# Routed expert tiles in half-tile slots (34 tiles instead of 36), and a new order in the end stage

## The chip, the core and the metric

The kernel runs on one core of one Trainium2 chip. The metric is the device time of one execution in microseconds; a run's time is the median of its executions. TensorE (PE) multiplies, and loads its stationary operand through a port of its own (PEld). VectorE (DVE), ScalarE (ACT) and GpSimd (POOL) work elementwise. SyncE (SP) issues most of the DMA transfers.

## What is computed

One transformer block on x of 2048 tokens by 512 features, all in float32. xn = layernorm(x). The output is x + attention(xn) + ffn(xn).

The attention is differential: 16 heads, two causal softmax maps for each head, a filter along the tokens by a real Fourier transform, a root-mean-square norm over each head, and a projection. The feed-forward part is a mixture of eight experts with two chosen for each token, and a shared expert of twice an expert's width:

```python
topk_w, topk_idx = jax.lax.top_k(scores, K)            # K = 2
topk_w = topk_w / jnp.sum(topk_w, axis=-1, keepdims=True)
h = jnp.einsum('th,ehi->eti', x, w1)                   # i = 352
g = jnp.einsum('th,ehi->eti', x, w3)
y_all = jnp.einsum('eti,eih->eth', jax.nn.silu(h) * g, w2)
...
shared = jax.nn.silu(x @ sw1) * (x @ sw3) @ sw2        # width 704
return y + shared
```

## The kernel before, in words

There are four stages. The first normalises the tokens, forms the values, and routes. Each token gets two slots, one for each of its experts. The slots of one expert stand together, in tiles of 128 (P); an expert's last tile may be partly empty. So 4096 slots and 8 experts need at most NS = 32 + 7 = 39 tiles. NR = 36 of them are always computed, and three more only under a condition (the branch on `more`). Which expert owns tile j is read at run time from `owner` (L452 to L458).

The second stage makes queries and keys and computes the shared expert for the first four token tiles.

The third, `middle`, is the long one. It interleaves two streams of work on PE by hand. One is attention: for each of eight head groups and four query chunks it does the scores (ps_s, L772), the exponentials on ACT (L785), the mask on POOL (L790), the products with the values (ps_o, L812), the sums of the probabilities on DVE (L829), and the closing steps (ps_sum, ps_ot, ps_st). The other is the generator `experts`, which first finishes the shared expert, then goes over the 36 routed tiles. A planner calls `work()` so often that the units of work done keep pace with the attention stream: it compares worked / (work_all - left) with the share of the stream, with left = 11.0.

For tile j the generator does, on PE, the transposition of the 128 gathered token rows (ps_x, L160), the two up products (xh in `up_first`, xg in `up_third`, both L169), the transposition of the gated result (ps_u, L192) and the down product (xy, L202). The down product of tile j stands one step later, after the xg of tile j + 1. ACT scales the result into y_sb (L211), and SP stores it in ys (L214).

The weights of an expert are 1408 KB for the up products (wu) and 768 KB for the down product (wd). There are two places for each. After the xg of tile j, SP issues the load of wu for tile j + 2 into the place just freed (L142); after the down product of tile j - 1, it issues wd for tile j + 1 (L145). After the last routed tiles the same places take the shared expert's weights for the last stage.

The last stage, `ending`, computes the shared expert for the last token tile (wh, L232; tanh into ws on ACT, L242; wy, L270), the filter's products (ps_r and ps_z, L1091) with additions on DVE, and the norm and the projection of 16 token tiles in eight pairs (`Pair`, `prepared`, ps_tr L1211, po L1219). The products of the filter beyond the first few need DVE's L1136 and L1137, which stand in DVE's order after the first ws of this stage. The program's memory is reused between stages: the first ws lies where buffers of `middle` lay. Gathers on POOL (L1075) add the two rows of ys of each token to the result.

DVE, PE, ACT, POOL and SP all run in the order in which the instructions stand, in `middle` and (without SP) in `ending`. "Tile j" below is the j-th routed tile; tiles count from 0.

Of the kernel before, what the change touches and what calls it, by code (L numbers as in the profile page):

```python
# [19 lines left out]
P = 128  # L20
# [22 lines left out]
NS = T * TOP // P + NX - 1  # L43
NR = NS - 3
# [13 lines left out]
C_ID, C_RANK, C_ROW, C_TOK = 0, 128, 136, 176  # L58
# [5 lines left out]
def block_kernel(  # L64
# [33 lines left out]
    rows = cst[:, C_ROW : C_ROW + NS]  # L98
# [4 lines left out]
    owner = cpool.tile([P, NS], I32, name="owner")  # L103
# [43 lines left out]
    def routed(j):  # L147
        return wex[bass.ds(nc.values_load(owner[0:1, j : j + 1], engines=[SP], min_val=0, max_val=NX - 1), 1)]

    def expert(mp, fps, yp=None, stores=2, by_scalar=False):  # L150
# [14 lines left out]
        def up_half(w, xT, i, name):  # L165
            dst = bank([P, FI], name)
            for c in range(NE):
                o = (2 * c + i) * FI
                nc.tensor.matmul(dst, xT[:, c, :], w[:, o : o + FI], start=(c == 0), stop=(c == NE - 1))  # L169
            return dst  # L170
# [27 lines left out]
        def down_products(pairs):  # L198
            y = bank([P, E], "xy")
            for n, (w, uT) in enumerate(pairs):  # L200
                for ic, (_, m) in enumerate(FCH):
                    nc.tensor.matmul(  # L202
                        y, uT[:m, ic, :], w[:m, ic * E : (ic + 1) * E],
                        start=(n == 0 and ic == 0), stop=(n == len(pairs) - 1 and ic == NF - 1),
                    )
            return y
# [9 lines left out]
        def down(pairs, *to):  # L216
            stored(down_products(pairs), *to)
# [61 lines left out]
    with ExitStack() as pools:  # L279
# [152 lines left out]
        nc.vector.tensor_scalar(n_int, before[:, NT, :], float(P - 1), None, ALU.add)  # L432
        nc.vector.tensor_scalar(n_int, n_int, -P, None, ALU.bitwise_and)
        ends = [l1.tile([P, NX], F32, name=f"ends{i}") for i in range(2)]
        nc.vector.tensor_copy(ends[0], n_int)
        cur = 0
        for d in (1, 2, 4):
            nc.vector.tensor_copy(ends[1 - cur][:, :d], ends[cur][:, :d])
            nc.vector.tensor_add(ends[1 - cur][:, d:], ends[cur][:, d:], ends[cur][:, : NX - d])
            cur = 1 - cur  # L440
        first = l1.tile([P, NX], F32, name="first")
        nc.vector.memset(first[:, 0:1], 0.0)
        nc.vector.tensor_copy(first[:, 1:], ends[cur][:, : NX - 1])
        at = l1.tile([P, NT, NX], F32, name="at")
        nc.vector.tensor_add(at, before[:, :NT, :], first.unsqueeze(1).to_broadcast([P, NT, NX]))
        for k in range(TOP):
# [3 lines left out]

        past = l1.tile([P, NS, NX], F32, name="past")
        nc.vector.tensor_tensor(  # L452
            past, rows.unsqueeze(2).to_broadcast([P, NS, NX]),
            ends[cur].unsqueeze(1).to_broadcast([P, NS, NX]), ALU.is_ge,
        )
        own = l1.tile([P, NS], F32, name="own")
        nc.vector.tensor_reduce(own, past, AX.X, ALU.add)
        nc.vector.tensor_scalar(owner, own, float(NX - 1), None, ALU.min)  # L458
        nc.vector.tensor_scalar(more, ends[cur][0:1, NX - 1 : NX], NR * P + 0.5, None, ALU.is_gt)

# [86 lines left out]
        for n, us in enumerate(chunks(xnT[:, :, : EARLY * P], u_last)):  # L547
            if n == 0:
                pm = lps.tile([P, 2, P], F32, tag="x", name="ps_most")
                for i in range(2):  # L550
                    nc.tensor.transpose(pm[:1, i, :], most[:, i : i + 1], ident)
                line = l1.tile([1, 2], F32, name="line")
                nc.vector.tensor_reduce(line, pm[:1], AX.X, ALU.max)
                prod = l1.tile([1, 1], F32, name="prod")
                nc.vector.tensor_mul(prod, line[:, 0:1], line[:, 1:2])
                nc.vector.tensor_scalar(calm, prod, BOUND / (D * SCALE), None, ALU.is_le)
        for t in range(EARLY):
            stored(result(us, t), ysh[t], 0.5, nc.gpsimd)

    def middle(general):  # L560


        with ExitStack() as pools:
# [29 lines left out]
            def experts():  # L593
# [7 lines left out]
                for t0 in range(EARLY, NT - 1, TQ):  # L601
# [24 lines left out]
                    if last:  # L626
                        es.append(routed(1))
                        fetch_up(es[1], 1, nc.sync)
# [11 lines left out]
                yield 0.6  # L640
                for j in range(NR):
                    if j > 0:
                        late = [(w_sb[(j - 1) % 2][1], turned_back(u))], ys[(j - 1) * P : j * P, :], wcol[:, j - 1 : j]
                    half = up_first(w_sb[j % 2][0], xT)
                    yield 2.9 if late else 2.4
                    u = up_third(w_sb[j % 2][0], xT, half)
                    if j + 2 < NR:
                        xr.append(rows_of(j + 2))

                    es.append(routed(j + 2) if j + 2 < NR else wex[NX + j + 2 - NR : NX + j + 3 - NR])  # L650
                    fetch_up(es[j + 2], j % 2, nc.sync)
                    yield 2.4
                    if j + 1 < NR:
                        xT = transposed(xr.pop(0))
                    if late:
                        down(*late)
                        fetch_down(es[j + 1], (j + 1) % 2, nc.sync)
                    if j == 1:
                        shared.append(True)
                    if late:  # L660
                        yield 3.2
                late = [(w_sb[j % 2][1], turned_back(u))], ys[j * P :][:P], wcol[:, j : j + 1]
                yield 0.5
                down(*late)
                yield 2.8
# [265 lines left out]
            work_all = (NT - 1 - EARLY) * ((2 * SCH - 1) * 3.45 / TQ + 5.2) + NR * 8.5  # L931
            left = 11.0
# [108 lines left out]
    def ending():  # L1041
# [3 lines left out]
        with tc.tile_pool(name="tail1", bufs=1) as t1, tc.tile_pool(name="tail", bufs=2) as tp, tc.tile_pool(  # L1045
# [110 lines left out]
            z = at(5, vd, 14)  # L1156
# [32 lines left out]
            def prepared(n):  # L1189

                z, i, by = ((z0, 0, 1.0), (z1, 2, ROOT), (z0, 1, COS8), (z1, 3, COS8 * ROOT))[n // 2]
                if n == 2:
                    nc.vector.tensor_sub(u0, u0, v0)
                    turned(z1, u0)
                elif n == 4:
                    scaled(v1[:, 0], dv[:, 1], TAN8, dv[:, 0])
                    scaled(v1[:, 1], dv[:, 0], -TAN8, dv[:, 1])

                    nc.vector.tensor_add(z0[:, 0], u1[:, 0], v1[:, 1])
                    nc.vector.tensor_sub(z0[:, 1], u1[:, 1], v1[:, 0])  # L1200
                elif n == 6:
                    nc.vector.tensor_sub(u1[:, 0], u1[:, 0], v1[:, 1])
                    nc.vector.tensor_add(u1[:, 1], u1[:, 1], v1[:, 0])
                    turned(z1, u1)
# [53 lines left out]
            nc.vector.tensor_sub(dv, z, dv)  # L1258
# [3 lines left out]
            for n in range(NT // 2):  # L1262
# [4 lines left out]
                if n == 0:  # L1267
                    stored(y, ysh[NT - 1], 0.5)
# [16 lines left out]
    with tc.If(nc.values_load(more[0:1, 0:1], min_val=0, max_val=1) > 0):  # L1285

        with tc.tile_pool(name="before_more", bufs=1) as gap, tc.tile_pool(name="more", bufs=2) as mp, tc.tile_pool(
# [4 lines left out]
            for j in range(NR, NS):  # L1292
                w = mp.tile([P, WCOL], F32, tag="w", name="w")
                nc.sync.dma_start(w, routed(j).rearrange("o p w -> p (o w)"))
# [11 lines left out]
                u = up(w[:, :WUP], transposed(x))  # L1306
                down([(w[:, WUP:], turned_back(u))], ys[j * P : (j + 1) * P, :], pairs[:, 1:])
# [11 lines left out]
def _tables():  # L1319
# [7 lines left out]
    cst[:, C_ROW : C_ROW + NS] = P * np.arange(NS)  # L1327
# [91 lines left out]
```

## Time and profile before

| | |
|---|---|
| median of 3 runs | 1362.34 us (1362.26 to 1364.04) |
| the profiled execution, its own time | 1361.8 us |
| its span | 1360.1 us |
| PE busy | 1322.2 us, 97% of the span |
| DVE, ACT, POOL busy | 1002.6, 691.8, 615.9 us |
| TensorE clock granted, mean | 0.996 |
| DMA | 206.65 MB, 152 GB/s mean |
| xh and xg (L169), 288 instructions each | 91.8 and 94.1 us busy |
| xy (L202), 216 instructions | 100.9 us busy |
| routed tiles, first xh to last xg | 598.1 to 1232.4 us of the span |

How to read it: a span is the time from the first to the last instruction that the profiler recorded. The execution's own time is 1.7 us longer. A float32 matrix product appears as two instructions for one of the program, so four products of 128x352 stand as x8. Matrix products are pipelined and their ends are modelled, so the start of one to the start of the next tells more than the length of one.

### The profile page before, as it was taken

The numbers are of one execution on the slowest core, as the hardware profiler recorded it, in microseconds if no ns is written. First come the engines' busy times: TensorE is split into PE (matmuls) and PEld (weight loads), VectorE is DVE, ScalarE is ACT, GpSimd is POOL, SyncE is SP. The second block draws the span as 40 slices with busy tenths as digits, with TensorE's granted clock in tenths as the row PEclk, the third lists the DMA queues.
The fourth block names the chain that finished last, engine by engine and source line by source line (L and its number), as shares of the span: only waits on it lengthen the run. The fifth ranks groups of instructions, "written<-read, shape, count | busy, mean of one in ns | idle before, by whom it ended". The sixth has DMA issues, their size and how long they took to land.

```text
span 1360.1 us, 20623 instructions
## 1 busy us (share of the span) xinstructions
PE 1322.2 (97%) x7480; PEld 613.6 (45%) x7480; DVE 1002.6 (74%) x1339; ACT 691.8 (51%) x853; POOL 615.9 (45%) x673
## 2 busy tenths in 40 slices
PE   7999999999999999999999999999999999998998
PEld 3444444333443444444444444444444454445544
DVE  7048882287668778767886878997788779776785
ACT  2311110265656566565666666666666666661321
POOL 0003420012220323227884986795369529731764
PEclk9999999999999999999999999999999999999999
DMA  9406662200210122236565666466566555557997
GB/s 378 175 16 177 200 202 90 89 12 31 67 52 30 38 77 80 75 114 182 180 216 168 197 192 191 148 211 202 164 183 215 193 178 182 179 169 259 191 223 153
DMA packets 75024, 206.65 MB, mean 152 GB/s; under 512 B 12200, under 2 KB 12656, under 8 KB 69536
## 3 DMA queue, kind: packets, MB, share of 16 engines
q1 hardware_dynamic: 62032, 177.56, 40.2%
q0 software_dynamic: 11216, 23.31, 8.5%
q10 hardware_dynamic: 1664, 4.36, 0.9%
q8 instruction: 62, 1.02, 0.3%
q14 instruction: 50, 0.41, 0.1%
HBM read 161.29 MB, written 43.89 MB: 151 GB/s over the span
## 4 chain that ended last, share of the span: by engine, by line
PE 65%; DVE 7%; POOL 5%; DMA 2%; issue 1%; ACT 1%; DVEq 0%; ACTq 0%; POOLq 0%
PE ps_o L812 16%; PE ps_s L772 12%; PE wh L232 9%; PE xy L202 6%; PE xg L169 6%; PE xh L169 5%; PE wy L270 4%; DVE sum L829 2%; PE ps_sum L838 2%; POOL pt L790 2%; DMA wu<-in_wex_dram 1%; PE ps_ot L850 1%; PE ps_u L192 1%; PE po L1219 1%; PE ps_x L160 1%
## 5 line engine op out<-in xcount | busy, mean ns | idle before, releaser
L829 DVE TENSOR_TENSOR sum<-sum,pt 128x1024 f32<-128x1024 f32 (+3 forms) x576 | 621.8, 1128 | 35.2 <-ACT pt L785 23.3
L785 ACT ACTIVATE pt<-ps_s 128x1024 f32<-128x1024 f32 x544 | 527.1, 1022 | 182.1 <-PE ps_s L772 125.7
L790 POOL TENSOR_SCALAR_AFFINE_SELECT pt<-pt 128x256 f32<-128x256 f32 x256 | 168.7, 683 | 385.5 <-ACT pt L785 372.0
L812 PE MATMUL ps_o<-pt,vd 128*32 128x512 f32 (+3 forms) x2560 | 268.4, 534 | 2.9 <-POOL pt L790 2.9
L772 PE MATMUL ps_s<-qS,kS 64*128 64x512 f32 (+3 forms) x1280 | 204.0, 406 | 1.7 <-DVEq L1285 1.6
L772 PEld LDWEIGHTS ps_s<-qS,kS 64*128 64x128 f32 x1280 | 97.4, 185 | 176.6 <-issue 98.3
L232 PE MATMUL wh<-xnT,wu 128*128 128x512 f32 (+1 forms) x352 | 151.9, 579 | 0.0
L812 PEld LDWEIGHTS ps_o<-pt,vd 128*32 128x32 f32 x2560 | 66.9, 109 | 124.8 <-issue 107.8
L522 PE MATMUL ps_x<-xnT,wqk_sb 128*128 128x512 f32 x256 | 110.5, 593 | 0.0
L202 PE MATMUL xy<-wd,uT 128*128 128x512 f32 (+1 forms) x216 | 100.9, 603 | 7.1 <-DVE rcp L853 7.1
L475 POOL DMA_INDIRECT who<-pairs,slot x32 | 33.7, 1053 | 141.8 <-DVE pairs L472 100.6
L232 PEld LDWEIGHTS wh<-xnT,wu 128*128 128x128 f32 x352 | 64.8, 191 | 73.2 <-issue 57.9
L169 PE MATMUL xg<-wu,xT 128*128 128x352 f32 x288 | 94.1, 470 | 0.0
L169 PE MATMUL xh<-wu,xT 128*128 128x352 f32 x288 | 91.8, 462 | 0.3 <-DMA wu<-in_wex_dram 0.2
L867 POOL TENSOR_TENSOR vd<-o_n 128x128 f32<-128x128 f32 x60 | 63.0, 1069 | 63.8 <-DVE o_n L858 63.7
L522 PEld LDWEIGHTS ps_x<-xnT,wqk_sb 128*128 128x128 f32 x256 | 48.4, 190 | 60.6 <-issue 60.6
L270 PE MATMUL wy<-wd,ws 128*128 128x512 f32 x160 | 74.9, 603 | 0.0
L169 PEld LDWEIGHTS xg<-wu,xT 128*128 128x128 f32 x288 | 51.9, 190 | 35.1 <-issue 10.4
L243 DVE SCALAR_TENSOR_TENSOR ws<-ws,wh 128x512 f32<-128x512 f32 (+4 forms) x26 | 16.7, 644 | 68.9 <-ACT ws L242 68.9
L539 ACT CAST hi<-turned 128x1024 fp32r<-128x1024 f32 x16 | 16.7, 1045 | 93.9 <-DVE turned L537 71.5
L1075 POOL DMA_INDIRECT res<-ys,slot x32 | 54.2, 1693 | 20.9 <-DMA res<-ysh 10.6
L169 PEld LDWEIGHTS xh<-wu,xT 128*128 128x128 f32 x288 | 51.9, 190 | 24.9 <-DVE rcp L853 1.7
(243 smaller groups left out, 1411.6 us busy)
## 6 DMA issues: line engine op xcount, KB each, us to landing
wu<-in_wex_dram SPq DMA_DIRECT2D x40, 1408.0 KB
wd<-in_wex_dram SPq DMA_DIRECT2D x39, 768.0 KB
kS<-parts_k SPq DMA_DIRECT2D x128, 128.0 KB
qS<-parts_q SPq DMA_DIRECT2D x256, 64.0 KB
ys<-y_sb SPq DMA_DIRECT2D x36, 256.0 KB
parts_q<-hi SPq DMA_DIRECT2D x32, 256.0 KB
parts_k<-hi SPq DMA_DIRECT2D x16, 256.0 KB
parts_k<-turned SPq DMA_DIRECT2D x16, 256.0 KB
```

The costliest lines, as they stand in the source:

```text
L169: nc.tensor.matmul(dst, xT[:, c, :], w[:, o : o + FI], start=(c == 0), stop=(c == NE - 1))
L202: nc.tensor.matmul(y, uT[:m, ic, :], w[:m, ic * E : (ic + 1) * E], start=(n == 0 and ic == 0), stop=(n == len(pairs) - 1 and ic == NF - 1),)
L232: nc.tensor.matmul(dst, w_sb[o // WUP][0][:, o % WUP : o % WUP + P], x[:, c, :], start=(c == 0), stop=(c == NE - 1))
L270: nc.tensor.matmul(y, us[i][:, t * P : (t + 1) * P], w_sb[i // NF][1][:, i % NF * E : (i % NF + 1) * E], start=(i == 0), stop=(i == SCH - 1),)
L522: nc.tensor.matmul(ps[:, i, :], wqk_sb[st, qk][:, i, c, :], xnT[:, c, cols], start=(c == 0), stop=(c == NE - 1),)
L772: nc.tensor.matmul(to, k, queries[2 * g + h, qc][r, off : off + w], start=True, stop=not general)
L785: nc.scalar.activation(pt[:, :, used], ps[:, :, used], AF.Exp, scale=SCALE)
L790: nc.gpsimd.affine_select(out=part, in_=part, pattern=[[0, 2], [1, P]], compare_op=ALU.is_ge, fill=0.0, base=0, channel_multiplier=-1,)
L812: nc.tensor.matmul(self.o[r : r + 32, off:], vd[:, kb, v0 : v0 + 32], pt[:, s, :], start=first, stop=self.ended, skip_group_check=True,)
L829: nc.vector.tensor_add(to, to, pt)
L867: eng.tensor_add(vd[:, self.qc * TQ : (self.qc + 1) * TQ, v0 : v0 + 32], self.o_n[:, :, h, 0, :], self.o_n[:, :, h, 1, :],)
L1075: nc.gpsimd.indirect_dma_start(out=came[k], out_offset=None, in_=ys, in_offset=bass.IndirectOffsetOnAxis(ap=slot[:, step - 2, order[k] : o ...
```

## The change

Slots are given out by half tiles of 64. An expert's slots fill whole tiles first; the remainder, if it is 64 or less, takes half a tile, and the half tiles of different experts share tiles behind all the whole ones. So 4096 slots and 8 experts need at most NS = (64 + 8) / 2 = 36 tiles, of which NR = 34 are always computed. At least NP = 28 of these hold one expert alone. Tiles 28 to 33 are treated as two halves, each with an owner of its own: both places of wu and of wd hold weights of the same tile, and each product becomes two, for rows 0 to 63 with the one set and 64 to 127 with the other. So 28 + 12 = 40 sets of weights are loaded.

The routing computes two ends for each expert, and the owner of 72 half tiles instead of 39 tiles. That computation is moved from the slot computation into the second step of the early shared expert. In `ending`, one subtraction (dv) is moved from the first pair to the step in which it is used, and the scaling and store of the last shared tile from the first to the second round. The load of the shared wd of place 0 is moved behind the last down product. The planner's `left` goes from 11.0 to 18.0, and work_all counts 34 tiles and 0.5 more for each of the six.

```diff
-NS = T * TOP // P + NX - 1
-NR = NS - 3
+HALF = P // 2
+NS = (T * TOP // HALF + NX) // 2
+NR = NS - 2
+NP = (T * TOP // HALF - NX) // 2
...
+        def parts_of(ws):
+            n = P // len(ws)
+            return [(slice(i * n, (i + 1) * n), w) for i, w in enumerate(ws)]
+
-        def up_half(w, xT, i, name):
+        def up_half(ws, xT, i, name):
             dst = bank([P, FI], name)
             for c in range(NE):
                 o = (2 * c + i) * FI
-                nc.tensor.matmul(dst, xT[:, c, :], w[:, o : o + FI], start=(c == 0), stop=(c == NE - 1))
+                for r, w in parts_of(ws):
+                    nc.tensor.matmul(
+                        dst[r, :], xT[:, c, r], w[:, o : o + FI], start=(c == 0), stop=(c == NE - 1),
+                        skip_group_check=True,
+                    )
             return dst
...
-        def down_products(pairs):
+        def down_products(ws, uT):
             y = bank([P, E], "xy")
...
+            for ic, (_, m) in enumerate(FCH):
+                for r, w in parts_of(ws):
                     nc.tensor.matmul(
-                        y, uT[:m, ic, :], w[:m, ic * E : (ic + 1) * E],
-                        start=(n == 0 and ic == 0), stop=(n == len(pairs) - 1 and ic == NF - 1),
+                        y[r, :], uT[:m, ic, r], w[:m, ic * E : (ic + 1) * E], start=(ic == 0), stop=(ic == NF - 1),
+                        skip_group_check=True,
                     )
...
-        nc.vector.tensor_add(at, before[:, :NT, :], first.unsqueeze(1).to_broadcast([P, NT, NX]))
+        nc.vector.tensor_tensor(at, before[:, :NT, :], over_tiles(whole), ALU.is_ge)
+        nc.vector.tensor_mul(at, at, over_tiles(first[:, 1]))
+        nc.vector.tensor_add(at, at, before[:, :NT, :])
+        nc.vector.tensor_add(at, at, over_tiles(first[:, 0]))
...
-                        es.append(routed(1))
+                        es.append(routed(2))
...
+                sets = [[j] if j < NP else [2 * j - NP, 2 * j - NP + 1] for j in range(NR)]
+                halves = [2 * j + i for j in range(NR) for i in range(len(sets[j]))]
...
                 for j in range(NR):
...
-                    es.append(routed(j + 2) if j + 2 < NR else wex[NX + j + 2 - NR : NX + j + 3 - NR])
-                    fetch_up(es[j + 2], j % 2, nc.sync)
+                    for n in sets[j]:
+                        m = n + 2 - len(halves)
+                        es.append(routed(halves[n + 2]) if m < 0 else wex[NX + m : NX + m + 1])
+                        fetch_up(es[n + 2], n % 2, nc.sync)
                     yield 2.4
                     if j + 1 < NR:
                         xT = transposed(xr.pop(0))
                     if late:
                         down(*late)
-                        fetch_down(es[j + 1], (j + 1) % 2, nc.sync)
+                        for n in sets[j - 1]:
+                            fetch_down(es[n + 2], n % 2, nc.sync)
...
                 yield 0.5
                 down(*late)
+                fetch_down(wex[NX : NX + 1], 0, nc.sync)
...
-            work_all = (NT - 1 - EARLY) * ((2 * SCH - 1) * 3.45 / TQ + 5.2) + NR * 8.5
-            left = 11.0
+            work_all = (NT - 1 - EARLY) * ((2 * SCH - 1) * 3.45 / TQ + 5.2) + NR * 8.5 + (NR - NP) * 0.5
+            left = 18.0
...
                 elif n == 4:
+                    nc.vector.tensor_sub(dv, zw, dv)
...
-            nc.vector.tensor_sub(dv, z, dv)
...
-                if n == 0:
+                if n == 1:
                     stored(y, ysh[NT - 1], 0.5)
```

## The prediction

> **What bounds the kernel now.** I read the page's busy times first, then the table of stages, then the waits, then the chain of work that ended last.
>
> ```profile
> PE 1322.2 (97%) x7480; PEld 613.6 (45%) x7480; DVE 1002.6 (74%) x1339; ACT 691.8 (51%) x853; POOL 615.9 (45%) x673
> ```
>
> ```profile
> 600.00:1232.00 632.00, 619.88 (x4278) 299.04 (x4277) 516.54 (x618) 407.49 (x496) 429.36 (x468) 1.00 0.59 185
> ...
> 1250.00:1360.00 110.00, 97.37 (x316) 49.90 (x316) 78.09 (x125) 26.93 (x42) 68.90 (x48) 0.98 0.93 195
> ```
>
> The columns are the stretch, its length, then busy time (and count) of PE, PEld, DVE, ACT and POOL, the clock, the DMA share and GB/s. While the routed tiles run, PE is busy for 619.9 of 632 us: an instruction less on PE there is time gained. From 1250 on DVE and PE lean on each other.
>
> One routed tile on PE, from the chain (start, us, what), with one piece of attention beside it for comparison:
>
> ```profile
> 1154.54 0.48 PE ps_u L192 x3
> 1155.02 2.37 PE xh L169 x8
> ...
> 1158.05 1.85 PE ps_o L812 x16
> ...
> 1160.56 2.56 PE xg L169 x8
> ...
> 1164.79 0.59 PE ps_x L160 x4
> 1165.38 2.58 PE xy L202 x6
> ```
>
> And the place where the routed tiles end:
>
> ```profile
> 1240.10 2.59 PE xy L202 x6
> ...
> 1242.77 0.69 ACT y_sb L211
> 1243.48 6.27 DMA ys<-y_sb
> ...
> 1249.93 0.39 ACT ws L242
> ...
> 1251.83 0.61 DVE vd L1137
> 1252.57 3.54 PE ps_z L1091 x4
> ```
>
> Here the path leaves PE: the last routed tile is stored, the store takes 6.27 us to land, and only then does ACT write the first ws (it lies in memory that the store still reads). DVE's L1137 stands behind ws, and PE's ps_z behind L1137. So whatever delays the last xy delays everything after it, although PE has other work.
>
> The loads of wu are seen by DMA traffic (1 us windows, same columns as above):
>
> ```profile
> 1164.00:1165.00 1.00, 1.00 (x11) 0.28 (x4) 1.00 (x2) 1.00 (x2) 0.91 (x2) 1.00 1.18 203
> 1165.00:1166.00 1.00, 1.00 (x6) 0.60 (x5) 1.00 (x2) 1.00 (x3) 1.00 (x1) 1.00 0.74 259
> 1166.00:1167.00 1.00, 1.00 (x4) 0.45 (x3) 0.92 (x1) 0.53 (x2) 1.00 (x2) 1.00 1.00 428
> 1167.00:1168.00 1.00, 1.00 (x5) 0.24 (x5) 0.00 (x0) 0.01 (x1) 0.18 (x1) 1.00 0.93 394
> 1168.00:1169.00 1.00, 1.00 (x11) 0.53 (x14) 0.00 (x0) 1.00 (x2) 0.00 (x0) 1.00 0.41 166
> ```
>
> This load was issued at 1163.16 and its last packet ended at 1169.0. The five from 1148 to 1214 took 5.5, 5.9, 7.5, 5.6 and 5.8 us from issue to last packet. It starts slowly (203, 259 GB/s) and then runs at about 0.41 MB/us; at the program's start, where many loads are queued, the windows show 0.39 to 0.44 throughout.
>
> **What the Trainium skill says.** "TensorEngine Tiling (Array Packing)", Theoretical Speedup and Key Properties: with at most 64 columns of the stationary operand two tiles of the array work side by side, up to twice the rate. No product here has 64 columns, but ps_o has 32: 16 instructions of 512 rows took 1.85 us, which is four passes of 0.46 and not sixteen of 0.43 (xy: 2.58 / 6). That agrees for four tiles. "DMA: Bandwidth & Descriptors", Queues, rings and completion order: descriptors are consumed in ring order. The trace agrees: a store issued on SP at 1237.74 moved its first packet at 1238.59, when a wu issued at 1232.46 had sent its last (1238.41). The same page, Bandwidth, has 341 GB/s for 1 MB and 425 for 16 MB; here a lone wu reaches 1.44 MB in about 4.8 us, 300 GB/s, and the queued ones 0.41 MB/us.
>
> **The change, part by part.** Let T be the end of the last xg on PE; before, T = 1232.4.
>
> *Two tiles less.* ps_u 0.48, xh 2.37, xg 2.37 to 2.56, ps_x 0.59, xy 2.58: 8.5 us of PE, twice: -17.0. All of it lies before T or moves there in kind.
>
> *Six tiles in halves.* Their products have twice the instructions with 64 columns, side by side. Each pass may cost up to what ps_o pays over xy, 0.46 against 0.43, or 7.6% of 7.4 us: 0 to 0.56 a tile. I take 0.5, most of it for 16 of 18 products before T: +2.7.
>
> *What stands before T.* In the changed order one group of ps_sum (0.88) and one of ps_ot and ps_st (0.75), which stood after the last xg, stand before it: +1.6. It is no gain or loss in itself, it shifts T.
>
> *Weights of the six tiles.* Both places of wu belong to one tile, so both loads (2.88 MB) are issued after its xg and needed at the next tile's xh. Between the two, the changed order has the attention pieces, ps_x, xy and ps_u: by the durations above 10.0, 10.4, 10.2, 9.7 and 10.4 us for the five gaps. The loads: 5.8 us for the first, 1.44 / 0.41 = 3.5 for the second, 0.2 to be seen, 9.5; a gather of 256 KB beside it adds 0.6 in four gaps, the filter's tables (1.5 MB, on ACT's queue) about 1 in the last. That is 0 to 0.4 us short in each gap, 0.6 in all; one load in five took 1.6 us longer. I take +2.0 (bounds 0 and 11). Behind these loads on SP wait the store of y_sb, the two wd and at times qS. The two wd have 16 us or more until used, except in the last tile.
>
> *The last tile.* This is what the change costs. Before, the wd of the last tile was fetched a tile ahead. Now both wd of tile 33 can be issued only after xy of tile 32, about T + 5, and stand on SP's ring behind both shared wu, issued at T. So: wu, wu 9.3; the store of tile 32 0.6; two wd 1.57 / 0.41 = 3.8: landed at T + 13.8. xy (2.75 with its halves) ends at T + 16.5. From there to ws it took 7.25 before (1242.68 to 1249.93), and the transfers in between are the same: ws at T + 23.8. Before it was 17.5. So +6.3. PE waits visibly: about 2 us for the shared wu in front of wh, and 6 in front of the last xy. DVE's folding of the last head group ended at T + 16.0 before and hides none of it. The shared wd of place 0, now issued on SP behind the last store, holds up nothing: its user wy ran at 1282, over 30 us later.
>
> *Routing.* In front: about 0.6 us more on DVE before the slots are known, hidden while PE makes queries (a unit is 6.95 us on PE and 5.7 on DVE). Owners: four operations of 128x576, by 0.47 us for 312 elements some 0.87 each, and small ones, 4 us, among steps of 3.45 us of PE in which DVE has half its time. Both 0; without cover 1 and 4.
>
> *End stage.* dv (1.21) and y_sb (0.68) move to later places on DVE, but both still stand before the `a` of pair 6, at whose end (1335.7) PE takes over and works without pause. DVE's sum is unchanged, so 0. PE gets two of the `a` earlier and waits longer for the next. If DVE's waits for ACT (3.5 us) shrank, it gains 1; if a PSUM bank held longer stalls PE, it loses 1.
>
> *Sum against the profiled execution.* -17.0 + 2.7 + 1.6 + 2.0 + 6.3 = -4.4; 1361.8 - 4.4 = 1357.4. The median of the runs stands 0.5 above the profiled one, so 1358.0.
>
> **Rivals.**
>
> *The tail is hidden* (chance 0.26). If the wd come beside the wu rather than behind them, or the pair loads run at the full rate from the first byte, the 6.3 falls to about 1 and the 2.0 to 1.5: -11.2 + 1 = about 1352. For it: the start-up rate of 0.42. Against: the ring order seen at 1237.74.
>
> *The pair loads come late: slower* (0.10). If the second wu is no faster than a lone one, the loads take 1.0 + 2 x 4.8 + 0.6 = 11.2, 12.2 with a start as slow as the 7.5 us load's: 2.2 over the gap of 10.0, five times, +11; and at the end a wu 1.3 and two wd 2.8 later, +4.1. Then -17.0 + 2.7 + 1.6 + 11.0 + 6.3 + 4.1 = +8.7: 1371. It decides the sign once the gaps lose over 1.8 us each (7.1 above my 2.0). For it: the lone loads. Against: the stream at the start.
>
> *Another stall takes the gain* (0.08). PE waits 13.2 us between 560 and 1240 for other reasons (7.1 for DVE's rcp before xy). The new pace moves each of these meetings; a few more give about 1362.
>
> *The halves don't run side by side* (0.03). Then xh, xg and xy of six tiles double: 6 x 7.4 = 44 more, about 1402.
>
> **How the numbers follow.** Likeliest, as summed: 0.53, its own range 1354 to 1361. A measurement tells about 0.2% of this kernel, 2.7 us, from no change, so faster means under 1359.6: 0.40 of the likeliest and all of the hidden tail, 0.66. Same: 0.13 of the likeliest and the 0.08: 0.21. Slower: 0.13. The range of 8 in 10 goes from 1350 (hidden tail, with the halves free) to 1365 (part of the late loads).
>
> **What would show it.** xh, xg and xy of tiles 28 to 33 as 16, 16 and 12 instructions in 2.4 to 2.6, 2.4 to 2.6 and 2.6 to 2.9 us; T near 1221.7; waits of xh for DMA wu of 2 us in all; PE waiting some 6 us for DMA wd in front of the last xy; ws 23 to 24 us after T; from ws to the end 110 us as before. It is wrong if the last xy doesn't wait, if the xh waits are over 7, or if the end from ws on changes by over 1.

## The result, and the profile after

The changed kernel takes 1359.88 us in the median of 17 runs, the kernel before 1362.34 in the same rounds. The ratio of the two is 0.9977 (95% interval 0.9969 to 0.9986): 3.1 us less, 1.9 to 4.2. One of the 17 runs took 5385 us and is left out of the ratio. The profiled execution took 1360.14 us, its span 1358.3.

The page's first line, then the stages (columns as before: stretch, length, busy time and count of PE, PEld, DVE, ACT, POOL, the clock, DMA share, GB/s):

```profile
PE 1312.6 (97%) x7554; PEld 600.3 (44%) x7554; DVE 1005.4 (74%) x1344; ACT 688.4 (51%) x847; POOL 626.3 (46%) x671
```

```profile
600.00:1232.00 632.00, 614.55 (x4393) 290.27 (x4390) 520.24 (x631) 403.29 (x491) 439.96 (x466) 0.99 0.62 196
1232.00:1250.00 18.00, 13.18 (x52) 6.92 (x51) 7.23 (x27) 1.55 (x3) 0.00 (x0) 0.96 0.71 269
1250.00:1358.00 108.00, 97.36 (x316) 49.79 (x315) 76.16 (x121) 26.15 (x40) 69.63 (x48) 0.98 0.95 200
```

PE is busy 9.6 us less in all, but the time fell by only 3: the rest came back as idle time. From 600 to 1232 PE stands idle for 17.5 us where it was 12.1, and after 1232 there are 4.8 us idle in 18. The chain shows where, with one tile in halves at its beginning (start, us, what):

```profile
1162.70 2.52 PE xg L180 x16
...
1168.99 2.73 PE xy L216 x12
...
1173.66 8.46 DMA wd<-in_wex_dram
1182.13 0.30 SPq L739
...
1184.46 10.78 DMA wu<-in_wex_dram
...
1195.28 4.27 PE xh L180 x14
...
1221.64 2.52 PE xg L180 x16
...
1229.57 8.55 DMA wd<-in_wex_dram
...
1238.16 2.81 PE xy L216 x10
...
1241.04 0.70 ACT y_sb L225
1241.76 5.25 DMA ys<-y_sb
...
1247.12 0.39 ACT ws L256
```

Two loads are on the path now. For tile 32 PE waits for a double load of wu, and for the last tile for a double load of wd. Twice as many instructions on half the columns take 2.52 us where 2.37 stood (xh, xg) and 2.73 where 2.58 stood (xy). T, the end of the last xg, is 1224.16 instead of 1232.43; ws begins at T + 23.0 instead of T + 17.5; and from ws to the end it is 111.2 us instead of 110.1.

In the next section times between marks of one profile (T, ws, the start of a product) are compared as well as medians. They carry a scatter of their own: up to the first xh the program is the same in the changed kernel and in all its variants, and it took 599.4 to 602.6 us in their profiles.

### The profile page after: what moved, and what is told of

Same layout as the page of the kernel before. It is cut to its first block, busy times and chain, and to the rows that moved or that the text cites. A ratio compares the mean times of both kernels' runs of the same rounds, so it can differ in the third digit from the quotient of the medians.

```text
span 1358.3 us, 20810 instructions
## 1 busy us (share of the span) xinstructions
PE 1312.6 (97%) x7554; PEld 600.3 (44%) x7554; DVE 1005.4 (74%) x1344; ACT 688.4 (51%) x847; POOL 626.3 (46%) x671
## 4 chain that ended last, share of the span: by engine, by line
PE 65%; DVE 6%; POOL 5%; DMA 3%; issue 1%; ACT 1%; SPq 0%; DVEq 0%; ACTq 0%; POOLq 0%
PE ps_o L862 16%; PE ps_s L822 12%; PE wh L246 8%; PE xy L216 6%; PE xg L180 5%; PE xh L180 5%; PE wy L284 4%; PE ps_sum L888 2%; DMA wu<-in_wex_dram 2%; POOL pt L840 1%; PE po L1270 1%; DMA wd<-in_wex_dram 1%; DVE sum L879 1%; PE ps_ot L900 1%; PE ps_x L165 1%
## 5 line engine op out<-in xcount | busy, mean ns | idle before, releaser
L216 PE MATMUL xy<-wd,uT 128*128 128x512 f32 (+3 forms) x240 | 97.1, 606 | 7.7 <-DVE rcp L903 6.3
L180 PE MATMUL xh<-wu,xT 128*128 128x352 f32 (+1 forms) x320 | 90.5, 473 | 4.2 <-DMA wu<-in_wex_dram 3.3
L180 PE MATMUL xg<-wu,xT 128*128 128x352 f32 (+1 forms) x320 | 88.6, 468 | 0.0
L180 PEld LDWEIGHTS xh<-wu,xT 128*128 128x128 f32 (+1 forms) x320 | 48.0, 176 | 31.7 <-issue 6.5
L180 PEld LDWEIGHTS xg<-wu,xT 128*128 128x128 f32 (+1 forms) x320 | 46.6, 174 | 34.4 <-issue 14.8
```

What stands on the lines that cost most here:

```text
L180: nc.tensor.matmul(dst[r, :], xT[:, c, r], w[:, o : o + FI], start=(c == 0), stop=(c == NE - 1), skip_group_check=True,)
L216: nc.tensor.matmul(y[r, :], uT[:m, ic, r], w[:m, ic * E : (ic + 1) * E], start=(ic == 0), stop=(ic == NF - 1), skip_group_check=True,)
```

## The experiments

The first four runs take the change apart. Twelve runs were made, all from the changed kernel; each was timed beside the kernel before, whose median was between 1361.4 and 1362.6.

### What two tiles less are worth, and what the second set of weights costs

34 whole tiles (whole34), and the same with the products of six tiles in halves but one set of weights for both halves (one_set). Both leave out the second expert's weights of those tiles and the line that loads wd behind the last down product:

```diff
-                sets = [[j] if j < NP else [2 * j - NP, 2 * j - NP + 1] for j in range(NR)]
-                halves = [2 * j + i for j in range(NR) for i in range(len(sets[j]))]
+                sets = [[j] for j in range(NR)]
+                halves = [2 * j for j in range(NR)]
...
-                    return [w_sb[n % 2][part] for n in sets[j]]
+                    return [w_sb[j % 2][part]]                            # whole34
+                    return [w_sb[j % 2][part]] * (1 if j < NP else 2)     # one_set
```

> 34 whole tiles: as one_set, but the last six tiles are also computed with the whole array at once (8, 8 and 6 instructions, one expert's weights; the second expert's weights are left out). Theory, a tile in halves costs 0.45 us over a whole one: 2.7 us under one_set, about 1344.5; against the kernel before it is two tiles of 8.5 less and 1.0 more in the end stage, 1346.3, so between 1344.5 and 1346.5. Rival, the halves cost nothing when PE is held by other engines: the same as one_set.

> The changed kernel, but the six tiles in halves fetch one expert's weights only and use them for both halves, so the second expert's weights are left out of the computation; products and instructions are those of the changed kernel. Theory, what the six tiles cost beyond 0.45 us each is the loads: xh's waits for wu go (7.2 us in all), the last tile's wd are fetched a tile ahead again, so ws comes at T + 17.5 instead of T + 23.0: 7.2 + 5.5 = 12.7 under the changed kernel, about 1347.2. Rival, the tail is covered (6.3 of the prediction isn't on the path): 7.2 less, about 1352.7. Second rival, the waits of xh only take the place of other waits of PE: 1355 or more.

Measured: whole34 1344.1 us, ratio 0.9872 (0.9857 to 0.9887), 17.4 us under the kernel before. one_set 1345.63, ratio 0.9876 (0.9861 to 0.9892). The intervals overlap, so the 2.7 us of the half products can't be read from the medians; from the first xh to T one_set takes 616.4 and whole34 614.0 us, 2.4 apart. PE waits for no weights in either. Against one_set the changed kernel (0.9977) loses 1.0%, 14 us. In the profiles it loses 6.9 from the first xh to T (623.3 instead of 616.4) and 8.6 from T to ws (23.0 instead of 14.4). So the theory holds, and the tail is not covered: the whole of what the second sets cost is on the path. The end of one_set follows. A line of this view has the start, the time, the engine (SPq and ACTq are the DMA queues of SP and ACT) and, in brackets, how long the engine stood idle before it and what ended that:

```profile
1218.43 0.33 SPq L146 DMA_DIRECT2D wu<-in_wex_dram  x1
...
1219.24 2.80 PE L216 MATMUL xy<-wd,uT 128*64 128x512 f32 x12
...
1223.12 2.80 PE L216 MATMUL xy<-wd,uT 128*64 128x512 f32 x12
...
1232.75 0.38 ACT L256 ACTIVATE ws<-wh 128x256 f32<-128x256 f32 x1 [6.05 <-DMA ys<-y_sb]
```

The last xy begins 4.7 us after T (1218.39 here), for its wd have been there for long; with two sets all but its first two instructions begin 14.0 us after T.

### Why the wait for wu costs more than it lasts

The change with 18 more transposes ahead of the wait (filler32):

```diff
-            for ic, (i0, m) in enumerate(FCH):
+            for ic, (i0, m) in [*enumerate(FCH)] * times:
...
-                        late = tile_down(j - 1, turned_back(u))
+                        late = tile_down(j - 1, turned_back(u, 7 if j == NR - 2 else 1))
```

> The changed kernel with work added: at the start of the second to last tile the three transposes into ps_u are made seven times over (18 more instructions, 2.4 us of PE), where PE waits 2.67 us for wu. Theory, the wait itself is only half of what that tile loses: after it the granted clock is 0.5 for some 3.4 us and xh runs at half speed (14 instructions in 4.27 us where 16 take 2.52 elsewhere). PE kept busy waits for wu under 0.5 us and its clock stays at 1.0: from the start of ps_u to the end of xh 5.6 to 6.4 us instead of 8.25, although there is more work, and the time falls by about 2. Rival, xh is slow because wu lands in pieces or the transfers take SBUF's bandwidth: xh stays above 4 us and the stretch at 8.2 or more.

First the changed kernel's PE at tile 32, then its clock (the third number from the end of a line):

```profile
1191.30 0.49 PE L206 MATMUL ps_u<-cst,xtanh 128*128 128x128 f32 x3
1191.81 0.81 PE L180 MATMUL xh<-wu,xT 128*64 128x352 f32 x2
1195.28 4.27 PE L180 MATMUL xh<-wu,xT 128*64 128x352 f32 x14 [2.67 <-DMA wu<-in_wex_dram]
```

```profile
1195.00:1196.00 1.00, 0.72 (x6) 0.37 (x8) 0.55 (x3) 0.00 (x0) 0.00 (x0) 0.94 1.03 428
1196.00:1197.00 1.00, 1.00 (x6) 0.45 (x4) 0.00 (x0) 0.00 (x0) 0.00 (x0) 0.50 1.01 424
1197.00:1198.00 1.00, 1.00 (x6) 0.47 (x3) 0.00 (x0) 0.00 (x0) 0.00 (x0) 0.50 0.65 270
1198.00:1199.00 1.00, 1.00 (x4) 0.23 (x1) 0.00 (x0) 0.00 (x0) 0.00 (x0) 0.50 0.09 37
```

And PE of filler32 in the same place:

```profile
1190.71 2.46 PE L206 MATMUL ps_u<-cst,xtanh 128*128 128x128 f32 x21
1193.10 0.81 PE L180 MATMUL xh<-wu,xT 128*64 128x352 f32 x2
1194.06 2.58 PE L180 MATMUL xh<-wu,xT 128*64 128x352 f32 x14 [0.15 <-DMA wu<-in_wex_dram]
```

From the start of ps_u to the end of xh 5.9 us instead of 8.25, with more work in it. The theory holds, with one term more. This xh of the changed kernel takes 5.2 us longer than the 2.52 of others: 2.67 are the wait, 1.7 the clock (4.27 instead of 2.58 for the same 14 instructions), and 0.9 the break in the product itself, which filler32 has too (3.54 from first to last, of which 0.15 is a wait). So little more than half of the loss is the wait. The median, 1358.41 (ratio 0.9982, 0.9971 to 0.9994), can't tell 2 us from none. The Trainium skill has this in "TensorE: Matmul & The Clock Gate", Part 1: the clock falls to half after an idle window of some 3.4 us and comes back after as long a busy one; the window runs freely. The trace agrees on the way back (half clock from about 1196 to 1199.2). The idle time was shorter here: 2.67 us were enough, and 2.34 before wh too (0.50 from 1230 to 1233), while a wait of 2.12 in another run, qs_later, left the clock at 1.0.

What tells these apart is where the wait lies. In all 14 profiles every change of the granted clock falls on a grid of 3.41 us; in the changed kernel, for example, 337.92 us lie between two changes, 99 times 3.413. From 560 us on the profiles have 3138 stretches of that grid at full clock. Each of the 36 in which PE is idle for more than 2.02 us is followed by half clock, and none in which it is idle for less than 1.83; in between both occur. (Near 253 us some fell after 1.6 already.) The 2.67 us before xh lie in one stretch; of the 2.34 before wh, 1.92 do; the 2.12 of qs_later are split into 1.22 and 0.90. So a stretch need not be idle throughout, as the page has it: a little over half of it is enough here.

### Why the wu of tile 32 are late

Two candidates: SP is held by the qS loads of the next attention turn (one head group and query chunk) and issues wu 1.2 us after their xg, or the token gather runs beside the load. The qS of the last turn on ACT's queue (qs_act), and on SP but four units, or steps, of attention later (qs_later):

```diff
-                            load_queries(*turns[n + 1])
+                            load_queries(*turns[n + 1], nc.scalar if n + 2 == len(turns) else nc.sync)   # qs_act
...
+                    if new:                                                                            # qs_later
+                        begun, due = n, 4 if n == len(turns) - 2 else 0
+                    if due == 0 and n + 1 < len(turns):
+                        load_queries(*turns[n + 1])
+                    due -= 1
```

> The changed kernel with the eight loads of qS for the last attention turn issued on ACT's queue instead of SP's; nothing else. Theory, SP is held by them for 8.3 us (each waits for an earlier transfer) and so issues the wu of the second to last tile 1.2 us after the xg that frees them: now they are issued within 0.2 us of it, the wait of 2.67 us shrinks to about 1.3, too short for the clock to drop, and from the start of ps_u to the end of xh it is 5.4 to 6.6 us instead of 8.25; the time falls by about 2. Rival, the load is late because of the gather beside it (it still takes 10 us from first to last packet): the stretch falls by 1.2 at most. Second rival, ACT is held in SP's place and PE waits for pt: the stretch gains, the time doesn't.

> The changed kernel with the eight qS loads of the last attention turn issued on SP four units of attention later, behind the wu of the second to last tile instead of ahead of them; no other queue takes them. Theory, SP held by qS was what made those wu late: they are issued at once behind their xg, PE's wait of 2.67 us is gone or under 0.6, the clock stays at 1.0, and from the start of ps_u to the end of xh it is 3.1 to 3.8 us instead of 8.25, with no PE wait for pt as when ACT issued them: T falls by some 4.5 and the time to about 1355.4. Rival, the gather beside the load keeps it late: the stretch stays above 5.5 and the time above 1357.5.

qs_act: 1364.67 us, ratio 1.0021 (1.0013 to 1.0030). The stretch from ps_u to the end of xh is 3.2 us and there is no wait for wu; but ACT is held in SP's place, and PE waits for the exponentials and then runs at half clock (the second rival). SP, ACT's queue and PE in qs_act:

```profile
1190.03 1.50 SPq L146 DMA_DIRECT2D wu<-in_wex_dram  x2
```

```profile
1173.68 7.73 ACTq L739 DMA_DIRECT2D qS<-parts_q  x6
1181.52 1.94 ACT L835 ACTIVATE pt<-ps_s 128x1024 f32<-128x1024 f32 x2 [6.95 <-DMA qS<-parts_q]
```

```profile
1182.60 1.71 PE L822 MATMUL ps_s<-qS,kS 64*128 64x384 f32 x8 [3.60 <-ACT pt L835]
```

This delay also put the gather (1188.7 to 1190.5) ahead of the load (from 1191.0), so qs_act doesn't tell the two apart. qs_later takes SP's delay away and leaves the gather: SP issues wu at once (xg ends at 1182.31) and still PE waits 2.95 us, 8.5 from ps_u to the end of xh. The median is 1361.29, ratio 0.9995 (0.9985 to 1.0005).

```profile
1182.33 1.49 SPq L146 DMA_DIRECT2D wu<-in_wex_dram  x2
1183.86 12.12 SPq L739 DMA_DIRECT2D qS<-parts_q  x8
```

```profile
1195.71 4.25 PE L180 MATMUL xh<-wu,xT 128*64 128x352 f32 x14 [2.95 <-DMA wu<-in_wex_dram]
```

Its load took 11.8 us from first to last packet with a gather beside it (1185.3 to 1189.6). So the theory fell: the load is late although SP issues it at once. The rival, the gather, is left, though here the qS loads had moved to behind the load. In the changed kernel the two double loads of routed weights with neither a gather nor the filter's tables beside them took 8.2 and 8.3 us; that of tile 32, with a gather at 1183.4 to 1186.3, took 10.4. Its traffic, and below it that of a load without a gather (first packet at 1130.3), same columns:

```profile
1184.00:1185.00 1.00, 1.00 (x8) 0.51 (x8) 0.39 (x1) 1.00 (x2) 0.49 (x2) 1.00 1.15 152
1185.00:1186.00 1.00, 1.00 (x6) 0.29 (x4) 0.90 (x2) 0.05 (x1) 0.00 (x0) 1.00 0.92 132
1186.00:1187.00 1.00, 1.00 (x6) 0.14 (x2) 0.90 (x1) 0.00 (x0) 0.00 (x0) 1.00 0.66 256
...
1131.00:1132.00 1.00, 1.00 (x10) 0.25 (x4) 1.00 (x2) 0.72 (x1) 1.00 (x1) 1.00 0.80 259
1132.00:1133.00 1.00, 1.00 (x9) 0.64 (x8) 1.00 (x2) 0.71 (x1) 0.92 (x2) 1.00 0.90 383
```

The DMA engines are busy (share 1.15 and 0.92) but move 132 to 152 GB/s, where a load without a gather moves 259 in its second us and 383 in its third. The Trainium skill's "DMA: Bandwidth & Descriptors", Queues, rings and completion order, says that each DMA engine takes turns between the queues that it has work for. The packet records add that the gather's 64 packets took 0.34 us each beside this load and 0.19 in qs_act, where the gather ran alone; 64 of 0.34 us over 16 engines make an estimate of 1.4 us.

The gather is not the whole of the 2.2 us. A packet of 16 KB on the queue of instruction fetches (q8) took 0.93 us of one DMA engine from 1192.1 on, and the last three of the load's 256 packets came 0.85 us behind the rest, one after another, as from one engine held up. In pairs_earlier, a run told below, two double loads with such a fetch and no gather (from 1121.3 and 1140.1) took 9.3 and 9.2 us, the last three packets 1.3 behind. And the load of tile 30 in the changed kernel, with a whole gather at its end and no fetch, took 9.0. By this comparison about 1 us of the 2.2 belongs to the fetch and about 1.2 to the gather; no run took either away alone. The rest of the 11.8 us of qs_later, which had both, isn't located.

### The tail

The fetch of the shared wu of place 1 moved behind the last down product (late_wu1):

```diff
-                        fetch_up(es[n + 2], n % 2, nc.sync)
+                        if m < 1:
+                            fetch_up(es[n + 2], n % 2, nc.sync)
...
                 down(*late)
+                fetch_up(es[-1], 1, nc.sync)
```

> The changed kernel, with the fetch of the shared wu of place 1 moved from behind the last xg to behind the last xy (it is first used some 45 us later). Theory, the wd of the last tile stand behind both shared wu on SP's ring: now only one wu is ahead of them, the two wd land at about 1234.3 instead of 1237.7, the last xy ends 3.5 us earlier (T + 13.3 instead of T + 16.8), ws comes at T + 19.5 instead of T + 23.0, and the time is 3.5 us under that of the changed kernel, about 1356.4. Rival, the tail is covered by other work or wh is what ends last there: within 1 us of the changed kernel, 1359 to 1360.5.

Measured: 1357.77 us, ratio 0.9978 (0.9969 to 0.9987), the ratio of the changed kernel. ws begins at T + 23.1 as before. The two wd are issued at T + 4.8 and landed at T + 12.9 instead of T + 13.6: with 1.44 MB less ahead of them they gain 0.7 us, not 3.4. The theory fell in its size. The traffic in late_wu1:

```profile
1228.00:1229.00 1.00, 1.00 (x6) 1.00 (x6) 0.93 (x6) 0.00 (x0) 0.00 (x0) 0.50 0.75 197
1229.00:1230.00 1.00, 1.00 (x7) 1.00 (x7) 0.93 (x6) 0.00 (x0) 0.00 (x0) 0.50 0.84 307
1230.00:1231.00 1.00, 1.00 (x7) 1.00 (x7) 0.93 (x6) 0.00 (x0) 0.00 (x0) 0.63 0.96 350
```

The wd run at 197 to 356 GB/s here and take 6.8 us for 1.57 MB. In the changed kernel, behind a full ring, they run at 418 to 430 and take 4.3. From issue to landing they take 8.1 us with little ahead of them and 8.8 with much. (The ring is the list of transfers issued on a queue and not yet moved.) So what sets the last xy is when wd can be issued, at the end of the xy before it. That PE waits for wd itself only 0.7 us hides this: wh stands ahead, waits for the shared wu and runs at half clock. In qs_later wh ran at full clock (3.84 us instead of 5.26); PE then waited 2.16 us for wd, and the last xy ended at T + 17.4, no earlier than the T + 16.8 of the changed kernel.

So the other remedy: two whole tiles last, the six in halves ahead of them (pairs_earlier).

```diff
+                seq = [*range(NP - 2), *range(NP, NR), NP - 2, NP - 1]
```

(sets, rows and tokens of tile j are then those of seq[j], and the last line that loads wd is dropped.)

> The changed kernel with the six tiles in halves worked on as tiles 26 to 31 of the order and two whole tiles last; nothing else. Theory, the tail is a matter of which tile comes last: the last tile's wd are fetched a tile ahead, ws comes at T + 14.4 to T + 17.5 instead of T + 23.0, which is 5.5 to 8.6 us; the waits of xh stay as they are up to some 2 us (five gaps with a double load as before): 1351.5 to 1354.5. Rival, T + 23 is set by the two shared wu and the order of wh on PE and not by the tile in halves: 1358 to 1360.

Measured: 1357.94 us, ratio 0.9976 (0.9967 to 0.9984). The tail is gone, ws begins at T + 14.0, 9.0 sooner after T. But T is 1229.2, 5.0 later, which takes more than half of that back, and the ratio shows none of the rest. xh waits 7.8 us for wu instead of 3.3, and longest in one gap:

```profile
1084.67 2.37 SPq L731 DMA_DIRECT2D kS<-parts_k  x4
1088.95 2.93 SPq L146 DMA_DIRECT2D wu<-in_wex_dram  x2
1091.93 18.93 SPq L743 DMA_DIRECT2D qS<-parts_q  x8
```

```profile
1107.30 1.40 PE L180 MATMUL xh<-wu,xT 128*64 128x352 f32 x2 [4.91 <-DMA wu<-in_wex_dram]
1110.58 3.98 PE L180 MATMUL xh<-wu,xT 128*64 128x352 f32 x14 [1.88 <-DMA wu<-in_wex_dram]
```

This double load took from 1090.0 to 1110.1, while the attention's keys and queries were loaded in the same stretch. Its qS moved behind the wd (pairs_qs_later, the edit of qs_later with 6 units and the third turn from the end):

> Two whole tiles last (as in the run with the halves earlier), with the qS loads of the third turn from the end issued on SP six units later, behind the store and the wd that stood behind them and ahead of the next double load. Theory, the waits of 4.9 and 1.9 us and the half clock behind them came from SP and the ring being full in that gap: they fall to under 2 us in all, T from 1229.2 to about 1221, ws stays at T + 14, and the time falls from 1357.9 to about 1350, under both kernels. Rival, the wu of that gap stand behind kS and qS of the turn before, which have not moved: the waits stay, 1356 or more.

1357.38 us, ratio 0.9967 (0.9955 to 0.9979). In that gap xh still waits 2.74 and 2.36 us, and T is 1230.1. The rival stands: moving these qS does not take the wait away, though the run doesn't show which of the other transfers of that stretch causes it. This is the fastest of the variants that load all the weights, but its interval overlaps that of the changed kernel; that it is faster is not shown.

### Halves between whole tiles

Each half tile followed by a whole one, from tile 21 of the order on, so that no two sets are needed at once:

```diff
+                seq = [*range(NP - 7), *(t for i in range(NR - NP) for t in (NP + i, NP - 7 + i)), NP - 1]
```

> The changed kernel with the six tiles in halves each followed by a whole one (whole tiles 0 to 20, then half, whole, half, whole and so on, the last two whole), nothing else: no tile needs two sets of wu that are both issued in the gap before it. Theory, both costs of the loads go, the waits of xh (7.2) and the late last xy (5.5 to 8.6), though the same bytes are moved: the time of the kernel with one set of weights, 1345.6, up to 1347. Rival, the bytes themselves (7.6 MB more) slow the other transfers: xh or xy still waits for DMA by several us, 1350 or more.

1379.77 us, ratio 1.0137 (1.0117 to 1.0158): far off. PE's waits between 600 and 1262:

```profile
PE xh L180 <- DMA wu<-in_wex_dram: 15.1, 1, 15.1
PE xy L216 <- DMA wd<-in_wex_dram: 11.4, 2, 6.3
```

In this order each set is needed one gap after its issue, where whole tiles in a row leave two, and at this point of the program the gaps hold keys as well as queries. SP just ahead of the wait of 15.1 us:

```profile
974.33 12.95 SPq L743 DMA_DIRECT2D qS<-parts_q  x8
987.32 2.32 SPq L731 DMA_DIRECT2D kS<-parts_k  x4
990.99 0.37 SPq L146 DMA_DIRECT2D wu<-in_wex_dram  x1
```

The xg that frees this wu ends at 978.8. SP is held for 15 us by queries and keys and issues the load 12.2 us later, and with their packets ahead of it its last ones land at 1005.7. The rival holds, and more strongly than it said. It also tells what the place of the six tiles is worth: in the changed kernel they come after the last keys have been loaded (1084.9 to 1087.2) and only two loads of queries fall among them.

### The end stage

The old order of dv and y_sb in the changed kernel (old_end), and ws with its two products behind the filter's first sums, with interleaved (inter_ws_later):

```diff
+            nc.vector.tensor_sub(dv, z, dv)          # old_end: in its first place again
...
-                if n == 1:
+                if n == 0:                           # old_end
                     stored(y, ysh[NT - 1], 0.5)
...
-            us = times(several((1, 3)), gated(several((0, 2))))
+            hs = several((1, 3)), several((0, 2))    # inter_ws_later
...
             nc.vector.tensor_sub(mid[:, 2:4], low[:, 0:2], z4)
+            us = times(hs[0], gated(hs[1]))
```

> The changed kernel with the end stage's old order (the subtraction for dv and the store of the last shared tile back in their first places). Theory, the new order holds a PSUM bank longer and PE waits 2.1 us for it (po behind res): that wait goes, ps_tr waits longer for a (4.0 instead of 2.7), from ws to the end it is 110.2 instead of 111.2 us, and the time falls by 1.0 to about 1358.9. Rival, the 1.0 us come from somewhere else (the clock, the transfers): from ws to the end stays at 111 and the time at 1359.9.

> As interleaved, and in the end stage the activation ws and the two products on it (which need the last tile's store to have landed) are put behind the first sums of the filter, so that neither ACT's first copy nor DVE's sums stand behind the store. Theory, with the tail gone it is this wait that ends last: the PE wait for vd before ps_z (2.1 us in the run with one set of weights) and the half clock that follows it go, 2 to 3.6 us under interleaved, about 1343. Rival, DVE's folding of the last head group ends as late as the store and the wait only changes its name: within 0.7 us of interleaved.

old_end: 1358.32 us, ratio 0.9977 (0.9967 to 0.9987). The wait of po is gone and that of ps_tr has grown, first in the changed kernel, then in old_end (us in total, times, longest):

```profile
PE ps_tr L1262 <- DVE a L1234: 2.7, 3, 1.3
...
PE po L1270 <- DVE res L1275: 2.1, 2, 1.9
```

```profile
PE ps_tr L1261 <- DVE a L1234: 4.5, 5, 1.9
```

The exchange of waits is shown; its net isn't. From ws to the end old_end takes 110.8 us, and the kernels with the new order, ws in its place, took 109.6 (qs_later) to 112.5 (whole34), so a difference of 0.4 from 111.2 says nothing.

inter_ws_later: 1377.41 us, ratio 1.0126 (1.0110 to 1.0143); from T to the end 124.8 us instead of 127.4. That looks like the 2 to 3.6 expected, but the next run has the same edit and no gain.

Both remedies and qS of the last three turns on ACT (moved_all):

> Two whole tiles last (as in the run with the halves earlier), the qS of the last three turns on ACT's queue, and ws behind the filter's first sums. Theory, the halves two tiles earlier lost in front what they gained in the tail because the eight qS loads on SP (18.9 us) held back a double load of wu (waits of 4.9 and 1.9 us and the half clock after them, about 8.5 in all): these go, T falls from 1229.2 to about 1220.5, ws' place gives 2.6 more, and the time is about 1346.5, under both kernels. Rival, the double load is late in that gap whatever SP does, because of the traffic of that stretch, or ACT's queue is held in turn: 1353 or more.

1374.62 us, ratio 1.0094 (1.0078 to 1.0109). xh's waits for wu fall from 7.8 to 2.2 us, as the theory said, but ACT is held by qS for up to 14.6 us and PE waits 20.1 us for the exponentials (10.8 the longest). And with ws out of the way another waits in its place:

```profile
1262.50 0.58 ACT L1187 COPY first<-ps_r 128x512 f32<-128x512 f32 x1 [7.30 <-DMA ys<-y_sb]
```

`first` needs the store too, so the wait has only changed its name; from T to the end it is 125.9 us, in pairs_earlier 125.3. No gain of this edit is shown.

## Why the prediction came out as it did, step by step

The forecast was 1358.0 (sum -4.4); measured were 1359.9, or 3.1 less by the ratio. The direction and the mechanism were right, two waits for weights eating most of two tiles; the sizes were partly off, and some reasons. That the sum came out so close is partly luck: T was 2.5 us later than forecast although the weights cost 5 more, ws came 0.8 sooner after T, and the end took 1.0 longer.

- *Two tiles less, -17.0.* whole34 is 17.4 under the kernel before, with the end stage's new order in it. Right.
- *Halves, +0.5 a tile.* 0.15 for each of xh, xg and xy, 0.45 a tile; 2.4 from one_set against whole34. Right; they run side by side, as the Trainium skill's "TensorEngine Tiling (Array Packing)", Theoretical Speedup, has it for up to 64 columns (2.52 us beside 2.37, not twice as long).
- *Weights of the six tiles, +2.0.* This is the term that was mis-sized: it cost about 7 (6.9 against one_set; 5.2 of it in tile 32, 1.6 in tile 33, 0.4 in tile 30). Without other traffic the double loads took what the sum had. What was missing: a gather beside the load was counted by its bytes, 0.6, and cost about 1.2 in tile 32's gap. An instruction fetch, about 1 there, wasn't in the sum. The qS loads were put behind the wu on SP and stand ahead of them in one gap, 1.2 (though qs_later shows that without this the wait stays). And what follows a wait, 1.7 of half clock and 0.9 for the break in the product, was not in the sum at all, though the trace of before had shown the half clock (0.50 from 1253 to 1255) after its wait of 3.4 before ps_z. The waits of xh alone were 3.3 us (forecast 2), far from the 7 that were to mean wrong; the loss of 7 counts what follows them too.
- *The last tile, +6.3.* The last xy began 14.0 after T (forecast 13.8) and ws at T + 23.0 (forecast 23.8), 5.5 more than before. Right in size. The reason given, that wd stand behind both shared wu, is the order on the ring but not what decides, as late_wu1 shows: with one wu less ahead, wd gained 0.7 us. Nor did the store of 1237.74, from which the ring order was read, show it: it moved its first packet 0.85 us after its issue, about as soon as the wu issued at 1163.16, which took 1.0. The changed kernel does show it: wd, issued at 1228.98, moved its first packet at 1233.41, when the last wu packet had ended at 1233.39. The 6 us of waiting before the last xy weren't seen as such: PE waited 2.34 for the shared wu, then did wh at half clock, and only 0.7 for wd were left.
- *T at 1221.7.* It was 1224.2. The terms above, with 7 for the weights, give 1226.7. PE waited 2.2 us less for two of DVE's results (rcp 0.8, xtanh 1.4) and 1.9 more for POOL and xT; the other 2.2 aren't located, and are within the scatter of the marks.
- *Routing, 0.* Right: before the first xh PE waits for the same results as in the kernel before, each within 0.2 us. The first xh comes at 600.9 instead of 598.2, with one more piece of attention ahead of it (912 instead of 896 instructions of ps_o).
- *End stage, 0 (plus or minus 1).* The mechanism named for the loss, a PSUM bank held longer, is there (po, 2.1 us) and ps_tr gained 1.3 on it. 111.2 instead of 110.1 is at the limit that was set, and not above the scatter.
- *The rivals.* The hidden tail fell (one_set, pairs_earlier), and the halves do run side by side. The slower case had its mechanism in part: one gap of five was late by 2.7 us, not all five.

## What to carry to other kernels

Work saved on the engine that bounds a kernel is worth what its new inputs leave of it: here 17.4 us were saved and 14 lost again to loads that two sets of weights had made a gap later. Cost a load by the gap in which it must land, with all that is issued ahead of it on its queue and all that runs beside it, and reckon with the half clock after any wait of PE over some 2 us. A wait moved to another queue or another place in the order is first of all a wait for someone else: in qs_act, pairs_earlier, old_end and moved_all another one took its place.

## What was not expected of the hardware

- Two waits of PE of like length end differently: after 2.12 us the clock stayed at 1.0, after 2.34 and 2.67 it was 0.5 for 3.4 us. What counts is the idle time within one stretch of a fixed grid of 3.41 us, here about 1.9 us of it.
- A small gather at the start of a large load: 132 to 152 GB/s in place of 259 to 383, with the DMA engines busy. One instruction fetch of 16 KB made a double load about 1 us longer, probably by holding up one of the DMA engines.
- A double load of wd (1.57 MB) took 4.3 us behind a full ring and 6.8 behind a nearly empty one.
- Eight loads of 64 KB hold the engine that issues them for 3.6 to 18.9 us on SP (before and pairs_earlier), and for up to 15.7 on ACT (moved_all): with loads in flight, the next issue waits until an earlier one has landed (in the changed kernel SP's qS waited 6.4 us for wd, as the chain shows at 1173.66).
